# A state space layer whose score products are paired and whose segment inputs become one stream

## The chip, the cores and the metric

The program runs on one core of one Trainium2 chip. A core has TensorE (PE in the profile; its weight loads are listed as PEld), VectorE (DVE), ScalarE (ACT), GpSimd (POOL) and a queue engine SyncE (SP) that mainly issues DMAs. The metric is the time of one execution in device microseconds. "Granted clock" is the share of TensorE's full clock that the profile shows as granted.

## The reference

A hybrid layer works on `x` of 2 sequences x 1024 tokens x 512 features, in float32. Four blocks follow one another, each as `x = x + block(layernorm(x))`: a state space layer, a mixture of experts, an attention, and the same mixture again. The change concerns the state space layer:

```
xBCzA = einsum('bld,ed->ble', input_, in_proj_w)      # 2048 channels, 1024 gates, 64 time steps
xBC   = silu(causal_conv(xBC, 4 taps) + conv1d_bias)  # -> x (64 heads x 16), Bm, Cm (8 groups x 64)
dt    = softplus(A_log)
Lm    = exp(segsum(A))                                # decay between tokens of a chunk of 128
Y_diag = einsum('bcshn,bczhn,bhcsz,bczhp->bcshp', Cm, Bm, Lm, X)
states = ...                                          # carried from chunk to chunk
Y_off  = einsum('bcshn,bchpn,bhcs->bcshp', Cm, states, state_decay_out)
Du     = D[None, None, :, None] * x_in                # x_in = x / dt
```

The sum of these is multiplied by the silu of the gates `z` and projected back to 512 features. The mixture that follows has 8 experts of which each token takes two, and a shared part.

## The kernel before

The 2048 tokens are 16 chunks of 128 (`CHUNKS`). Two chunks form a segment of 256 tokens (`SEG`, `CPS = 2`), so there are 8 segments, four per sequence.

`segment_inputs` (L546) makes all that a segment's chunks need. It is a generator: each `yield` ends a step, and there are 27 (`INPUT_STEPS`). Its steps are: the LayerNorm of two token tiles, their transposes on TensorE and their copies into `xnT`, all in one step; the time steps (`ps_dt`, L563, and then a chain of about 15 small VectorE instructions, L572 to L593, the "dt chain"); the decays (`ps_cum`, `ps_row`), with the cumulative sums written to DRAM (`sums`); then 16 steps of four projection matmuls for a channel tile (`ps_ch`, L631), convolved by four VectorE instructions that read PSUM (L634, L638), and 8 steps for a gate tile (`ps_z`, L656, silu on ScalarE, L660). Projections share three PSUM banks (tag `proj`). Their weights `w_ch` come by SP in pairs of tiles, with three buffers.

`prologue(c)` (L687), in three steps, transposes a chunk's x and B, makes `xd` and `y` on GpSimd, adds the output of the former chunk's state, and makes the next state.

`scores(c)` (L767) multiplies B by C for all 8 groups into two PSUM tiles `g0` and `g1` and masks them.

`own(c, gs, between)` (L781) is a chunk's main part. It takes the 64 heads as 8 groups of 8, in two halves `e` of 4 groups. For one group, SP broadcasts a stretch of `sums` to all partitions (tile `m`, 512 KB, six buffers), GpSimd subtracts (L799), ScalarE does relu and exp (L801, L802), VectorE multiplies by the scores (L803), and TensorE does 8 products with 32 output rows each (`ps_y`, L807; the profile lists each float32 product as two instructions, so 16 per group). After each group there is a `yield`. When four groups are done, four more matmuls add `y` (L818) and VectorE multiplies by the gate into `yT` (L826). Both halves use one PSUM bank `y`. After the first half, `between` runs, which is the prologue of the next chunk. At the end come `scores(c + 1)` and the output projection `ps_out` (L833), which is added to x.

The loop at the end of the layer (L885) runs `own` step by step. With each step it adds `rate` to `due`, and for each whole unit it runs one step of `side`, the generator of the next segment's inputs. When a new segment is due, `before_chunk` runs `side` to its end and starts the next one. In the second sequence every other step also runs a step of `routes`: LayerNorm and router of the first sequence for the mixture, 8 tiles of 5 steps and then the routing itself.

The text order is not yet the order on the engines. The framework's planner orders each engine's instructions at compile time: it takes the earliest written instruction that by its own estimate is ready, gives out buffers and sets the waits. On the chip each engine then works in that fixed order. SP's DMAs stand in one queue, where one that waits for a buffer holds back those behind it.

At the start, `load_x` asks SP for the 8 tiles of the first sequence, ahead of all else. LayerNorm's statistics are VectorE instructions (L154, L155), the reciprocal root is GpSimd's (L158, L159), and the normalised tile `xn` VectorE's (L180).

Of the kernel before, what the change touches and what calls it, by code (L numbers as in the profile page):

```python
# [11 lines left out]
F32 = mybir.dt.float32  # L12
# [26 lines left out]
INPUT_STEPS = 3 + (NCH + DI) // P  # L39
CHUNK_STEPS = 12  # L40
# [48 lines left out]
def hybrid_layer_kernel(ctx: ExitStack, tc: tile.TileContext, a: dict, out: bass.AP):  # L89
# [14 lines left out]
    load_x(range(TPB))  # L104
# [26 lines left out]
    def count(shape, pattern, base, channel_multiplier, name):  # L131

        whole = ints.tile(shape, I32, name=name + "_i")
        nc.gpsimd.iota(whole, pattern=pattern, base=base, channel_multiplier=channel_multiplier)
        c = const.tile(shape, F32, name=name)
        nc.vector.tensor_copy(c, whole)
        return c
# [373 lines left out]
    with ExitStack() as sa:  # L511
# [15 lines left out]

        convw = wp.tile([P, NCH // P, TAPS], F32, name="convw")
# [7 lines left out]
        w_dt = wp.tile([P, KD, NH], F32, name="w_dt")  # L536
        nc.scalar.dma_start(out=w_dt, in_=a["wdt"])
# [8 lines left out]
        def segment_inputs(b, s, before):  # L546
# [5 lines left out]
            else:  # L552
                nc.gpsimd.tensor_copy(xnT[:, :, 0:HALO], before[:, :, SEG : SEG + HALO])
            for j in range(CPS):
                transposed(normalised(b, s * CPS + j, stats[j]), pp, "misc", xnT[:, :, HALO + j * P : HALO + (j + 1) * P])

# [13 lines left out]
            n = CPS * NH  # L570
            al = sp.tile([P, n], F32, tag="al", name="al", bufs=1)
            nc.vector.tensor_copy(al, ps_dt.rearrange("p c h -> p (c h)"))  # L572
            y = sp.tile([P, n], F32, tag="sp_y", name="sp_y", bufs=1)
            nc.vector.scalar_tensor_tensor(y, al, -1.0, al, ALU.mult, ALU.min)
            nc.scalar.activation(y, y, AF.Exp)
            r = sp.tile([P, n], F32, tag="sp_r", name="sp_r", bufs=1)
# [4 lines left out]
            s2 = sp.tile([P, n], F32, tag="sp_s2", name="sp_s2", bufs=1)  # L581
# [81 lines left out]
            for n, quad in enumerate((2, 3, 0, 1)):  # L663
                yield from channels(quad)
                yield from gates(n)
# [5 lines left out]
        for i in range(2):  # L671
            xc = wp.tile([P, NH // 2, 3, HP], F32, name=f"xc{i}")
            nc.gpsimd.memset(xc[:, :, 1, :], 0.0)
# [107 lines left out]
        def own(c, gs, between):  # L781


            b, s, j = place_of(c)
            cum, sums, gate = (segs[c // CPS][i] for i in (3, 4, 8))
            cols = slice(j * P, (j + 1) * P)
            xc = xcs[c % 2]
            y = started.pop(c)
            yT = cp.tile([P, 2, 4, P], F32, tag="wide", name="yT", bufs=4)
            for e in range(2):  # L790
                ps = pp.tile([P, 4, P], F32, tag="y", name="ps_y", bufs=1)
                for i in range(4):
                    h0 = (2 * i + e) * 8
                    m = cp.tile([P, 8, P], F32, tag="m", name="m", bufs=6)
                    nc.sync.dma_start(
                        out=m.rearrange("p h s -> p (h s)"),
                        in_=sums[j][h0 * P : (h0 + 8) * P].partition_broadcast(P),
                    )
                    nc.gpsimd.tensor_tensor(m, m, bc(cum[:, j, h0 : h0 + 8], 2, P), ALU.subtract)  # L799

                    nc.scalar.activation(m, m, AF.Relu)  # L801
                    nc.scalar.activation(m, m, AF.Exp, scale=-1.0)  # L802
                    nc.vector.tensor_tensor(m, m, bc(gs[e][:, i, :], 1, 8), ALU.mult)  # L803
                    for odd in range(2):
                        for quad in range(4):
                            hh = quad * 2 + odd
                            nc.tensor.matmul(  # L807
                                ps[quad * 32 : (quad + 1) * 32, i, :],
                                padded(xc, h0 + hh),
                                m[:, hh, :],  # L810
# [376 lines left out]
```

## Time and profile before

| | us |
|---|---|
| three runs, median (lowest to highest) | 2377.78 (2375.65 to 2384.19) |
| the profiled execution | 2371.49 |
| its span, first to last instruction | 2369.7 |
| granted TensorE clock, mean | 0.976 |
| end of the last `ps_out` of the state space layer | 812.9 |

The times of the profile are microseconds from the start of the span. A row of the timeline has the start, the length, engine, line, operation, what is written and read, the shape and how many instructions were joined; in brackets stands how long the engine was idle before it and what ended that. Consecutive matmuls overlap in these rows by about 0.1 us, so the time from one start to the next start is the measure of cost. A row of busy time by stretch has the stretch, its length, the busy time and number of instructions of PE, PEld, DVE, ACT and POOL, the granted clock, the busy share of the DMA engines, and GB/s. Where it is asked for PE alone, only PE stands there.

### The profile page before, as it was taken

The page shows a single profiled execution, that of the slowest core. Times are in us where ns is not written, and L with a number is a line of the kernel's source. Part 1 is how long each engine was busy: PE and PEld are TensorE (multiplying, and loading weights), DVE is VectorE, ACT ScalarE, POOL GpSimd, SP SyncE. Part 2 cuts the span into 40 slices and gives each one's busy share as a digit, 9 for nine tenths or more (in the row PEclk, how much of TensorE's full clock was granted, in tenths as well). Part 3 has the DMA queues.
Part 4 walks back from the last instruction along what each step waited for, and adds up shares of the span by engine and source line. Part 5 has one row for each costly group of instructions (what it writes and reads, how often), then busy time and mean ns, then how long its engine had stood idle before and what let it go on. Part 6 is the DMA issues. An engine that isn't in the chain of part 4 may idle for free.

```text
span 2369.7 us, 29938 instructions
## 1 busy us (share of the span) xinstructions
PE 2237.8 (94%) x10996; PEld 1445.1 (61%) x10996; DVE 1418.6 (60%) x2117; ACT 860.9 (36%) x1416; POOL 1100.2 (46%) x757
## 2 busy tenths in 40 slices
PE   7999999999999999999889999999899998889998
PEld 6766767676776565655556556556556554556654
DVE  6867777777676530012249989884699899710002
ACT  4656576666566422211222223221223322212221
POOL 3443454455646300002377887744788886110002
PEclk9999999999999999999999999999999999989999
DMA  7444554454555487876744463344565553378775
GB/s 262 155 145 147 164 177 151 137 191 144 174 170 193 163 268 258 299 258 218 254 146 166 162 230 132 131 153 165 199 237 200 180 179 123 119 261 291 281 265 156
DMA packets 119314, 456.42 MB, mean 193 GB/s; under 512 B 17281, under 2 KB 20097, under 8 KB 106369
## 3 DMA queue, kind: packets, MB, share of 16 engines
q1 hardware_dynamic: 91904, 387.03, 47.0%
q0 software_dynamic: 12480, 40.90, 5.6%
q10 hardware_dynamic: 14784, 26.58, 3.1%
q8 instruction: 88, 1.44, 0.2%
q14 instruction: 58, 0.47, 0.1%
HBM read 408.84 MB, written 45.61 MB: 192 GB/s over the span
## 4 chain that ended last, share of the span: by engine, by line
PE 65%; DVE 11%; POOL 9%; DMA 6%; ACT 5%; issue 3%; POOLq 0%; ACTq 0%; SPq 0%; DVEq 0%
PE ps_o L470 13%; PE ps_u L448 11%; PE ps_g L439 11%; PE ps_ch L631 6%; PE ps_out L833 5%; POOL pr L1005 4%; PE ps_z L656 3%; DMA m<-sums 2%; PE ps_xnT L186 2%; PE ps_y L807 2%; POOL m L799 2%; DVE sc L1009 2%; PE ps_ao L1041 2%; DMA part<-made,r_slots 2%; DVE pv L1025 2%
## 5 line engine op out<-in xcount | busy, mean ns | idle before, releaser
L1005 POOL TENSOR_TENSOR pr<-qk 128x1536 f32<-128x1536 f32 x128 | 440.7, 3459 | 85.9 <-DVE sc L1009 55.3
L799 POOL TENSOR_TENSOR m<-m,cum 128x1024 f32<-128x1024 f32 x128 | 243.2, 1908 | 327.9 <-DMA m<-sums 215.9
L449 DVE TENSOR_TENSOR h<-h,ps_u 128x352 f32<-128x352 f32 x156 | 80.6, 517 | 493.3 <-PE ps_u L448 484.8
L376 POOL DMA_INDIRECT xg<-normed,r_tok x92 | 89.8, 976 | 531.5 <-PE ps_xnT L186 461.9
L631 PE MATMUL ps_ch<-xnT,w_ch 128*128 128x259 f32 x1024 | 263.1, 404 | 12.9 <-DVE chan L638 12.0
L470 PE MATMUL ps_o<-w_d,hT 128*128 128x512 f32 x552 | 257.9, 601 | 6.7 <-ACT hT L462 6.7
L1009 DVE TENSOR_REDUCE sc<-pr 128x32 f32<-128x1536 f32 x128 | 224.4, 1753 | 50.6 <-POOL pr L1005 50.6
L439 PE MATMUL ps_g<-w_gu,xT 128*128 128x352 f32 x736 | 238.1, 463 | 1.1 <-DMA w_gu<-in_wall 0.9
L448 PE MATMUL ps_u<-w_gu,xT 128*128 128x352 f32 x736 | 236.6, 462 | 0.0
L441 ACT ACTIVATE h<-ps_g 128x352 f32<-128x352 f32 x156 | 72.4, 464 | 449.0 <-PE ps_g L439 443.7
L631 PEld LDWEIGHTS ps_ch<-xnT,w_ch 128*128 128x128 f32 x1024 | 194.5, 197 | 61.2 <-issue 28.8
L801 ACT ACTIVATE m<-m 128x1024 f32<-128x1024 f32 x128 | 134.5, 1054 | 198.7 <-POOL m L799 198.5
L439 PEld LDWEIGHTS ps_g<-w_gu,xT 128*128 128x128 f32 x736 | 138.1, 191 | 93.5 <-issue 35.6
L476 ACT COPY y<-ps_o 128x512 f32<-128x512 f32 x92 | 53.9, 586 | 376.7 <-PE ps_o L470 376.7
L470 PE MATMUL ps_o<-s_d,hT 128*128 128x512 f32 (+1 forms) x384 | 182.1, 606 | 4.6 <-DVE x L473 3.8
L638 DVE SCALAR_TENSOR_TENSOR chan<-ps_ch,convw,chan 128x256 f32<-128x256 f32 x384 | 181.7, 478 | 7.5
L470 PEld LDWEIGHTS ps_o<-w_d,hT 128*128 128x128 f32 x552 | 105.8, 193 | 115.2 <-issue 88.1
L448 PEld LDWEIGHTS ps_u<-w_gu,xT 128*128 128x128 f32 x736 | 133.6, 192 | 60.9 <-issue 4.9
L439 PE MATMUL ps_g<-s_gu,xT 128*128 128x352 f32 x512 | 169.4, 464 | 0.6 <-ACT h L441 0.6
L448 PE MATMUL ps_u<-s_gu,xT 128*128 128x352 f32 x512 | 165.4, 461 | 0.0
L803 DVE TENSOR_TENSOR m<-m,g 128x1024 f32<-128x1024 f32 x128 | 150.9, 1215 | 19.8 <-ACT m L802 19.5
L1025 DVE TENSOR_TENSOR pv<-sc,vT 128x1024 f32<-128x1024 f32 x128 | 155.9, 1218 | 1.1
(211 smaller groups left out, 3548.5 us busy)
## 6 DMA issues: line engine op xcount, KB each, us to landing
w_gu<-in_wall SPq DMA_DIRECT2D x92, 1408.0 KB, 7.8
w_d<-in_wall SPq DMA_DIRECT2D x92, 768.0 KB, 4.6
m<-sums SPq DMA_DIRECT2D x128, 512.0 KB, 4.8
w_ch<-in_wch SPq DMA_DIRECT2D x96, 512.0 KB, 4.1
made<-y ACTq DMA_DIRECT2D x92, 256.0 KB, 6.0
xT<-columns SPq DMA_DIRECT2D x64, 256.0 KB, 5.0
s_gu<-in_wall SPq DMA_DIRECT2D x7, 1408.0 KB, 6.7
normed<-xn SPq DMA_DIRECT2D x32, 256.0 KB, 2.4
```

Of the source, the lines that this page charges most:

```text
L439: nc.tensor.matmul(ps_g, xT[:, k, :], both[:, k, 0, :], start=(k == 0), stop=(k == KD - 1))
L448: nc.tensor.matmul(ps_u, xT[:, k, :], both[:, k, 1, :], start=(k == 0), stop=(k == KD - 1))
L470: nc.tensor.matmul(ps_o, hT[:hn, c, :], wd[:hn, c, :], start=(c == 0), stop=(c == len(HC) - 1))
L631: nc.tensor.matmul(ps, w[:, ct % 2, k], xnT[:, k, :], start=(k == 0), stop=(k == KD - 1))
L638: nc.vector.scalar_tensor_tensor(c[:, i], ps[:, tap : tap + SEG], convw[:, ct, tap : tap + 1], c[:, i], ALU.mult, ALU.add)
L799: nc.gpsimd.tensor_tensor(m, m, bc(cum[:, j, h0 : h0 + 8], 2, P), ALU.subtract)
L801: nc.scalar.activation(m, m, AF.Relu)
L803: nc.vector.tensor_tensor(m, m, bc(gs[e][:, i, :], 1, 8), ALU.mult)
L833: nc.tensor.matmul(ps_out, yT[:, e, i, :], w_out[:, 2 * i + e, :], start=(e == 0 and i == 0), stop=(e == 1 and i == 3),)
L1005: nc.gpsimd.tensor_mul(pr, bc(qks[t][:, 0, i : i + IC, :], 2, AH), bc(qks[t][:, 1], 1, IC))
L1009: nc.vector.tensor_reduce(scores[t][:, i : i + IC, :], products.pop((t, i)), AX.X, ALU.add)
L1025: nc.vector.tensor_tensor(pv, bc(scores[t][:, i : i + IC, :], 2, DH), bc(vs[t], 1, IC), ALU.mult)
```

## The change

Four things are changed in the state space layer.

`own` is rewritten around runs of two groups, four runs to a chunk. `decayed(c, n)` makes the two tiles `m` of run n; `from_scores(c, n)` does the 32 score instructions of that run in one go. `decayed` is called one run ahead, so run 0 of chunk c + 1 is made in chunk c, and `scores(c + 1)` moves ahead of the last run of chunk c. A chunk now has 16 steps instead of 12.

The inputs of all segments are chained to one stream `side`. `before_chunk` no longer empties it, it only makes sure that the segment is there. By the first turn of a segment the stream is six steps (`LEAD`) further. LayerNorm becomes a step of its own, ahead of the transposes.

At the start, two tiles of x are asked for instead of eight; the six others come when the first segment's steps have reached number 10, the second sequence as before after that. `w_dt` is the first on ScalarE's DMA queue instead of the last. 22 transposes of the identity (`WARM`) go to TensorE ahead of the stream.

Four small casts go from VectorE to GpSimd, and two memsets of `xcs` from GpSimd to VectorE.

```diff
-INPUT_STEPS = 3 + (NCH + DI) // P
-CHUNK_STEPS = 12
+INPUT_STEPS = 4 + (NCH + DI) // P
+CHUNK_STEPS = 16
+LEAD = 6
+WARM = 22
...
-    load_x(range(TPB))
+    load_x(range(CPS))
...
-        nc.vector.tensor_copy(c, whole)
+        nc.gpsimd.tensor_copy(c, whole)
...
+        w_dt = wp.tile([P, KD, NH], F32, name="w_dt")
+        nc.scalar.dma_start(out=w_dt, in_=a["wdt"])
         convw = wp.tile([P, NCH // P, TAPS], F32, name="convw")
...
-        def segment_inputs(b, s, before):
+        def segment_inputs(b, s, before, n):
...
+            rows_before[n] = xnT
+            xns = [normalised(b, s * CPS + j, stats[j]) for j in range(CPS)]
+            yield
+
             for j in range(CPS):
-                transposed(normalised(b, s * CPS + j, stats[j]), pp, "misc", xnT[:, :, HALO + j * P : HALO + (j + 1) * P])
-
+                transposed(xns[j], pp, "misc", xnT[:, :, HALO + j * P : HALO + (j + 1) * P])
             yield
...
-            nc.gpsimd.memset(xc[:, :, 1, :], 0.0)
+            nc.vector.memset(xc[:, :, 1, :], 0.0)
...
+        def decayed(c, n):
+            cum, sums = segs[c // CPS][3:5]
+            j = c % CPS
+            ready[c, n] = []
+            for i in (n % 2 * 2, n % 2 * 2 + 1):
+                e = n // 2
+                h0 = (2 * i + e) * 8
+                m = cp.tile([P, 8, P], F32, tag="m", name="m", bufs=6)
+                nc.sync.dma_start(
+                    out=m.rearrange("p h s -> p (h s)"),
+                    in_=sums[j][h0 * P : (h0 + 8) * P].partition_broadcast(P),
+                )
+                nc.gpsimd.tensor_tensor(m, m, bc(cum[:, j, h0 : h0 + 8], 2, P), ALU.subtract)
+                nc.scalar.activation(m, m, AF.Relu)
+                nc.scalar.activation(m, m, AF.Exp, scale=-1.0)
+                nc.vector.tensor_tensor(m, m, bc(raw[c][e][:, i, :], 1, 8), ALU.mult)
+                ready[c, n].append(m)
+                yield
+
+        def from_scores(c, n):
+            ...
+            for i, m in zip((n % 2 * 2, n % 2 * 2 + 1), ready.pop((c, n))):
+                for odd in range(2):
+                    for quad in range(4):
+                        hh = quad * 2 + odd
+                        nc.tensor.matmul(
+                            ps[quad * 32 : (quad + 1) * 32, i, :],
+                            padded(xc, (2 * i + e) * 8 + hh),
+                            m[:, hh, :],
+                            ...
+                        )
+            if n % 2 == 1:
+                ...
+                nc.vector.tensor_tensor(finished[c][:, e], ps, gate[e][:, :, j * P : (j + 1) * P], ALU.mult)
...
+        def own(c, between):
+            finished[c] = cp.tile([P, 2, 4, P], F32, tag="wide", name="yT", bufs=4)
+            for n in range(4):
+                if n < 3:
+                    yield from decayed(c, n + 1)
+                elif c + 1 < CHUNKS:
+                    raw[c + 1] = scores(c + 1)
+                    yield from decayed(c + 1, 0)
+                from_scores(c, n)
+                yield
+                if n == 1:
+                    yield from between
+            project_out(c)
+            yield
...
-        for _ in inputs(0):
-            pass
+        warm = pp.tile([P, 4, P], F32, tag="y", name="warm", bufs=1)
+        for i in range(WARM):
+            nc.tensor.transpose(warm[:, i % 4], ident, ident)
+
+        side = chain(*(inputs(n) for n in range(CHUNKS // CPS)))
+        for n in range(INPUT_STEPS):
+            next(side)
+            if n == 10:
+                load_x(range(CPS, TPB))
...
-        gs = scores(0)
-        side = inputs(1)
-
-        rate = INPUT_STEPS / (CHUNK_STEPS + CHUNK_STEPS // 2 - 2)
+        raw[0] = scores(0)
+        for _ in decayed(0, 0):
+            pass
+        rate = (INPUT_STEPS + LEAD) / (CHUNK_STEPS + 6)
         due = 0.0
...
                 if c % CPS == 0:
-                    for _ in side:
-                        pass
-                    n = c // CPS + 1
-                    side = inputs(n) if n * CPS < CHUNKS else iter(())
+                    while c // CPS not in segs:
+                        next(side)
                     rate = INPUT_STEPS / (CPS * CHUNK_STEPS)
-                    due = 0.0
                 yield from prologue(c)
```

## The prediction

> **What bounds the kernel now.** I read the page first, then the state space part (roughly the first 815 us) in stretches, then TensorE's waits, then single places of the timeline. The page, and the table of busy time by stretch (60:740 is the steady part, 740:815 its tail, the rest is the later layers):
>
> ```profile
> span 2369.7 us, 29938 instructions
> PE 2237.8 (94%) x10996; PEld 1445.1 (61%) x10996; DVE 1418.6 (60%) x2117; ACT 860.9 (36%) x1416; POOL 1100.2 (46%) x757
> 0.00:60.00 60.00, 44.58 (x190) 37.90 (x191) 37.69 (x100) 27.06 (x31) 18.07 (x31) 0.97 0.77 261
> 60.00:740.00 680.00, 646.98 (x4788) 477.27 (x4787) 500.18 (x876) 428.12 (x491) 335.41 (x233) 0.98 0.48 159
> 740.00:775.00 35.00, 27.97 (x229) 17.27 (x226) 24.69 (x27) 20.88 (x25) 24.85 (x14) 0.87 0.61 223
> ```
>
> TensorE sets the time: in 60:740 it is busy 647 of 680 us, VectorE 500, ScalarE 428, GpSimd 335. So the change can win only idle TensorE time (33 us there), clock not granted, and busy time that is not multiplication. Places where each shows (start, length, engine, line; what a pause waited for):
>
> ```profile
> 11.13 1.00 DVE L180 TENSOR_SCALAR xn<-x,mv,rstd 128x512 f32<-128x512 f32 x2
> 11.73 1.97 PE L186 MATMUL ps_xnT<-ident,xn 128*128 128x128 f32 x8 [11.73 <-DVE xn L180]
> 13.52 3.68 PE L563 MATMUL ps_dt<-w_dt,xnT 128*128 128x64 f32 x16
> 16.99 9.52 PE L631 MATMUL ps_ch<-xnT,w_ch 128*128 128x259 f32 x32
> 31.33 7.17 PE L631 MATMUL ps_ch<-xnT,w_ch 128*128 128x259 f32 x32
> ...
> 79.64 3.33 PE L631 MATMUL ps_ch<-xnT,w_ch 128*128 128x259 f32 x14
> 82.90 0.64 PE L807 MATMUL ps_y<-m,xc 128*32 128x128 f32 x16
> ...
> 329.16 0.64 PE L807 MATMUL ps_y<-m,xc 128*32 128x128 f32 x16
> 329.74 2.02 PE L631 MATMUL ps_ch<-xnT,w_ch 128*128 128x259 f32 x8
> 331.69 0.64 PE L807 MATMUL ps_y<-m,xc 128*32 128x128 f32 x16
> ...
> 446.15 1.75 DVE L574 SCALAR_TENSOR_TENSOR sp_y<-al 128x128 f32<-128x128 f32 x1
> 446.74 5.53 PE L631 MATMUL ps_ch<-xnT,w_ch 128*128 128x259 f32 x24
> 455.25 3.60 PE L631 MATMUL ps_ch<-xnT,w_ch 128*128 128x259 f32 x8 [2.99 <-DVE chan L638]
> 747.39 1.95 PE L807 MATMUL ps_y<-m,xc 128*32 128x128 f32 x64
> ...
> 455.10:458.50 3.40, 3.25 (x8) 0.50 0.01 2
> ```
>
> To be seen: TensorE starts at 11.73; the same 32 matmuls take 9.52 us at first and 7.17 later; score products (ps_y) alternate with projections (ps_ch); when a segment begins, ps_ch waits for VectorE, and the 8 matmuls after that pause take 3.60 instead of 2.02 at a granted clock of 0.50.
>
> **The change part by part.** The sum is against the profiled execution: 2371.49 us, 1.79 more than its span. The median of three runs, 2377.78, is 6.29 higher; I carry the difference over to it.
>
> *Start.* Tile 0's statistics begin at 3.66 and both tiles' are done by 5.42, but GpSimd holds the next step (L159, 9.18) behind the statistics of a tile that lands later. With two tiles asked for, L159 (0.70 for two columns) can follow L158 at 5.8, xn (0.53) at 6.5, and TensorE at 7.1 instead of 11.73: 4.6 us. Four casts (0.15 to 0.22 each on VectorE) go to GpSimd and two memsets (0.97 for both) leave it; its constants end at 3.5, so they lie ahead of L158. SP issued eight x tiles for 5.98 us ahead of the first w_ch (6.84); now two, some 1.5 us. The other six come behind the fourth w_ch, which waits for a buffer; VectorE first needed tiles 2 and 3 for the next segment at 30.25; uncovered they would cost one landing, about 4 us. w_dt goes from last to first on ScalarE's queue, 2.84 us earlier, hidden. Ends 2 and 4.6; I take 4.
>
> The 22 warming transposes (eight took 1.97, so 5.4 us) fit between ident at 1.5 and 7.1. They could give back the slow start: 16 ps_dt took 3.68 at first and 1.27+0.88 for 10 and 6 later, less 0.1 overlap each; with 9.52-7.17 that is 1.6+2.3=3.9. Ends 0 and 3.9; I take 3. **Start: -7.**
>
> *Two groups in a run.* A score group alone takes 329.74-329.16=0.58; four in a run take 749.27-747.39=1.88. So a group costs 0.43 and a run 0.15 on top. Projections: 14 between two score groups take 82.90-79.64=3.26, 8 take 331.69-329.74=1.95; so 0.218 each and 0.20 per block. One switch less saves 0.35 us. There are 16 chunks x 8 = 128 groups, so at most 64 merges, 22 us; around each prologue groups already join (30 and 24 in the rows after 346), and there prologue matmuls may still cut a run. Ends 0 (other work cuts every run) and 22; I take 48 merges, near the upper end, because most runs in the timeline hold one group (91 of 123, counted): **-17**.
>
> *One run ahead, stream six steps ahead.* The matmuls are the same. Idle in 60:740 is 680-646.98=33 us. Clock: half in 171.8 to 175.2, 250.3 to 253.7, 352.7 to 359.5, 455.1 to 458.5, 533.6 to 537.0, 554.1 to 557.5, 642.8 to 649.6, together 30.6 us, so 15 lost. Together 48, nearly all within 25 us behind a segment's turn. There the flush of the old stream, LN, transposes, dt chain and the prologue come together: VectorE has both yo and the dt chain, GpSimd xd, y, state and m. After the change LN and dt are due 4 to 7 yields before that prologue, and projections are left as cover beside it; LN on VectorE gets a step of its own ahead of its transposes. What stays: the dt chain still stands ahead of the convolutions on VectorE, and ps_ch has three banks. That wait alone is 12.0 us of the 33. Ends 0 and 48 won; nor is a loss excluded, since one more pause as at 455 (2.99 and 1.7 of clock) per segment turn is 7x4.7=33. I take half of it, **-24**: the waits for ACT and POOL results in the prologue go, those for VectorE's chain stay. Late next is the dt chain.
>
> One rule weighs against this. The Trainium skill, "SBUF — State Buffer", section "SBUF: two separate sides", says that VectorE and GpSimd take turns at a shared port pair, whole instructions long. The trace agrees: L574 took 1.75 us beside a GpSimd subtraction, its shortest is 0.29. By the rule the chain is as slow wherever GpSimd subtracts; an estimate by it alone is half of this part, -12, and a sum of -34. Another rule, "TensorE: Matmul & The Clock Gate", section "What's actually happening", puts half clock behind an idle window of about 3.4 us; here 1.2 us before 352.7 was enough. By that rule only the 4.8 us pause before 171.96 would cost clock, 1.7 instead of 15, so this part would be half of 35 and the sum -39; the measurement decides.
>
> *New waits.* A run stands on TensorE until both m are multiplied; behind it wait projections, and on VectorE the convolutions wait behind an m that is late. Chain for one m: landing 4.8, L799 1.9, L801 and L802 2.1, table 1.28, L803 1.2 = 11.3. Six buffers hold three runs; at 11 us a run (45 per chunk) that is some 22 us of lead. Nothing, as long as queueing stays under ten.
>
> *Tail.* The stream ran out in chunk 13's first half; it now ends after chunk 12 (34 steps in 22 yields, then 0.875 each: yield 207 of 16 per chunk). Routing moves on every second yield and a chunk has 16 instead of 12, so it ends in chunk 13 instead of 15. Chunks 13 to 15 have GpSimd's 8x1.90+1.93+1.93+2x1.28+2x1.06=23.7 against TensorE's 7.1+3.8+2.1+1.8+1.2+1.6+1.1=18.7: up to 5 idle each, 15. Against that the present tail already idles 7.0 in 740:775, and later layers' ps_g moved in at 781. Ends -7 and +15; **+2**.
>
> Sum: -7-17-24+2=-46; 2371.5-46=2325.5, on the median **2332 us**.
>
> **The rivals.** *Turns stay as they are* (the DVE chain and port hold the 48 us): -7 and 8 to 17 of the switches, tail worse by 2 to 8: about 2362. For it: the 12.0 us wait; against: prologue waits that a lead must shorten. *Everything goes*: -8-22-40-7=-77, 2301; against it the same wait. *Slower: a run's second m is late.* GpSimd already waited 215.9 us for m to land, landings took up to 10.1. If TensorE stands before each run, 64 runs, gains of 46 are gone at 0.72 us each; at 1.2 us with its clock it ends near 2410. Against: ps_y waited only 2.2 us in all. *The order isn't what the text says*: instructions here are ordered by a planner (ps_ch of one block stand in 6 and 2 around ps_out), which could cut runs: then -29, 2349, inside my range.
>
> **How the numbers follow.** Forecast, with cut runs: 0.66, own range 2306 to 2358. Turns stay: 0.15 (2350 to 2372, a third of it above 2366). Everything goes: 0.07. Slower: 0.12, of it 0.02 within 0.5%. Half a per cent, 12 us, is about what a measurement here can tell. Faster 0.66+0.10+0.07=0.83, same 0.05+0.02=0.07, slower 0.10. Range 2300 to 2368: it leaves out the slower case and about half of the largest gain and a little of the second.
>
> **What would show it.** First PE matmul besides warm ones near 7 us, 32 ps_ch in 7.2 us; ps_y in runs of 32; ps_ch's wait for VectorE around 6 to 12 us; fewer half-clock stretches between 60 and 700; the last ps_out 46 us earlier than 812.9, with what follows as long as now. I am wrong if ps_y waits for m in most chunks, if runs are cut, or if the tail from the last ps_ch on idles over 20 us.

## The result and the profile after

The changed kernel takes 2408.49 us (median of four runs, 2397.56 to 2411.54); the kernel before 2376.72 (median of four, 2370.18 to 2384.19). The ratio is 1.0124, with a 95% interval of 1.008 to 1.0168: about 30 us slower (1.2%), where 46 us less were forecast. The profiled execution took 2409.57, with a span of 2407.4, 37.7 above the span before.

From the page after, TensorE's granted clock in tenths (40 slices of 60 us):

```profile
PEclk9999999999996899999999999999999999989999
```

The clock line has a dent in its thirteenth and fourteenth slices, 720 to 840 us: the end of the state space layer. Busy time by stretch after, all engines, in the columns of the prediction's table:

```profile
60.00:740.00 680.00, 620.97 (x4688) 467.09 (x4686) 486.34 (x870) 430.32 (x489) 319.85 (x229) 0.98 0.49 156
740.00:775.00 35.00, 22.91 (x156) 19.15 (x156) 20.57 (x37) 15.24 (x17) 21.24 (x12) 0.54 0.37 127
```

In 60:740 TensorE has 26 us less to do (646.98 before) and stands still for 59 us instead of 33. In 740:775 it has half its clock.

Fixed stretches compare unlike work, so the rest of this text cuts the run at two events: the end of the input stream (the last `ps_ch` or `ps_z`) and the end of the layer (the last `ps_out`). The same view, for TensorE alone, from 60 to the first event and from there to the second. Before:

```profile
60.00:726.50 666.50, 634.73 (x4638) 0.98 0.48 159
726.50:812.90 86.40, 78.12 (x645) 0.90 0.45 159
```

After:

```profile
60.00:732.90 672.90, 615.73 (x4576) 0.98 0.49 155
732.90:838.50 105.60, 83.54 (x667) 0.74 0.40 137
```

The stream ends 6.4 us later, the tail is 19.2 longer, and what follows the layer takes 1568.9 instead of 1556.8, 12.1 more. These three make the 37.7. In the first stretch idle time rose from 31.8 to 57.2, busy time fell by 19.0; the clock there stayed as it was (30.7 us at half clock both times). In the tail idle time rose by 13.8 and busy time by 5.4.

**New waits in the steady part.** What ended TensorE's idle time in 60:740 after (engine, operation, line, what it waited for: total, times, longest):

```profile
PE ps_ch L636 <- ACT gate L665: 16.3, 6, 3.9
PE ps_z L661 <- issue: 12.6, 5, 3.4
...
PE ps_ch L636 <- DVE chan L643: 3.5, 1, 3.5
```

Before, the last of these and the first read:

```profile
PE ps_ch L631 <- DVE chan L638: 12.0, 6, 4.8
...
PE ps_ch L631 <- ACT gate L660: 0.9, 2, 0.5
```

The wait that the list puts down to VectorE's convolutions fell, from 12.0 to 3.5, and a wait for ScalarE's gates came. But the five waits of `ps_z` for which the list names nothing ("issue", 12.6 us) belong to VectorE too: each ends 0.10 us after a convolution of VectorE's that stands right behind a step of the dt chain. The one at 355.70, in the timeline after:

```profile
354.93 0.27 DVE L591 SCALAR_TENSOR_TENSOR sp_r<-sp_r,sp_s 128x128 f32<-128x128 f32 x1
355.13 0.47 DVE L643 SCALAR_TENSOR_TENSOR chan<-ps_ch,convw,chan 128x256 f32<-128x256 f32 x1
...
355.70 1.97 PE L661 MATMUL ps_z<-xnT,w_ch 128*128 128x256 f32 x8 [2.10 <-issue]
```

With these, and with 6.1 us in which the transposes of `xnT` wait for the addition of `ps_out` to x (L853), all of TensorE's waits for VectorE up to the stream's end come to 22.7 us, where the kernel before had 21.9. What is new is ScalarE: 16.3 us for its gates (0.9 before) and 15.6 for its other results (7.2 before). One of the six waits for the gates, in the timeline after:

```profile
309.43 1.06 ACT L805 ACTIVATE m<-m 128x1024 f32<-128x1024 f32 x1 [3.41 <-POOL m L803]
311.29 1.06 ACT L805 ACTIVATE m<-m 128x1024 f32<-128x1024 f32 x1 [0.80 <-POOL m L803]
...
313.31 1.28 ACT L647 ACT_TABLE_LOAD   x1
...
315.56 0.82 ACT L665 ACTIVATE gate<-ps_z,zb 128x256 f32<-128x256 f32 x2
316.07 3.70 PE L636 MATMUL ps_ch<-xnT,w_ch 128*128 128x259 f32 x8 [3.17 <-ACT gate L665]
```

ScalarE works through its instructions in a fixed order. It stands for 3.41 and 0.80 us at the relu of tiles `m` that GpSimd has not subtracted yet (GpSimd has just worked on `xd` and `y` of the prologue, from 303.71 to 307.5); the silu of two gate tiles stands behind them; so two of the three projection banks stay full, and TensorE waits 3.17 us for one and runs the next eight matmuls in 3.70 us instead of about 2.

**The tail.** Timeline after, from the end of the stream:

```profile
733.00 1.95 PE L823 MATMUL ps_y<-m,xc 128*32 128x128 f32 x64
...
737.06 1.08 PE L823 MATMUL ps_y<-m,xc 128*32 128x128 f32 x32
748.74 1.08 PE L823 MATMUL ps_y<-m,xc 128*32 128x128 f32 x16 [10.60 <-DVE m L807]
```

GpSimd and SP's queue in the same place:

```profile
733.70 6.47 SPq L799 DMA_DIRECT2D m<-sums  x6
741.64 11.17 POOL L803 TENSOR_TENSOR m<-m,cum 128x1024 f32<-128x1024 f32 x6 [12.56 <-DMA m<-sums]
```

In about 5 us TensorE uses up the six tiles that stood ready. All six buffers are then asked for anew within 6.5 us, and TensorE stands 10.6 us for the first. Its clock falls to half and stays there; busy time and clock of TensorE in two stretches:

```profile
742.80:780.30 37.50, 26.39 (x182) 0.50 0.40 134
783.80:800.80 17.00, 14.74 (x87) 0.50 0.20 63
```

In these 54.5 us TensorE is busy for 41.1; by estimate half of that, 20.6 us, is due to the clock. The tail before has 17.0 us of half clock with 14.7 busy, so 7.4. The clock then costs some 13 us more than before, beside the 13.8 us of idle time.

### The profile page after: what moved, and what is told of

Read it like the earlier page. It is cut to its first block, busy times and chain, and to the rows that moved or that the text cites. A ratio compares the mean times of both kernels' runs of the same rounds, so it can differ in the third digit from the quotient of the medians.

```text
span 2407.4 us, 29968 instructions
## 1 busy us (share of the span) xinstructions
PE 2244.0 (93%) x11018; PEld 1464.5 (61%) x11018; DVE 1417.2 (59%) x2115; ACT 869.8 (36%) x1420; POOL 1100.2 (46%) x759
## 4 chain that ended last, share of the span: by engine, by line
PE 61%; DVE 11%; POOL 10%; DMA 7%; ACT 6%; issue 5%; SPq 0%; POOLq 0%; ACTq 0%; DVEq 0%
PE ps_o L472 12%; PE ps_u L450 11%; PE ps_g L441 11%; PE ps_ch L636 6%; POOL pr L1035 4%; DMA m<-sums 4%; PE ps_out L845 3%; PE ps_z L661 3%; PE ps_xnT L188 2%; DVE sc L1039 2%; POOL m L803 2%; DVE pv L1055 2%; PE ps_ao L1071 2%; PE ps_y L823 2%; DVE o L1056 2%
## 5 line engine op out<-in xcount | busy, mean ns | idle before, releaser
L636 PE MATMUL ps_ch<-xnT,w_ch 128*128 128x259 f32 x1024 | 258.4, 399 | 22.9 <-ACT gate L665 16.5
```

Of the source, the lines that this page charges most:

```text
L636: nc.tensor.matmul(ps, w[:, ct % 2, k], xnT[:, k, :], start=(k == 0), stop=(k == KD - 1))
```

## The experiments

Part of the change was undone, or done alone on the kernel before. "Points" are hundredths of the time before, from the ratios; the table after the last experiment has all numbers. Each kernel has one profiled execution, and that can lie up to 11 us from the kernel's median, so differences of a few us between two traces say little by themselves.

**The stream's lead taken back** (after):

```diff
-LEAD = 6
+LEAD = 0
```

> The changed kernel with LEAD = 0: the stream no longer runs six steps ahead at a segment's turn, all else as changed. Theory T (the loss is in the last three chunks, which have no filler left): the stream lasts seven steps of the loop longer, so the tail is shorter by under half a chunk: about 2395 to 2400 us, and the pause of 10.6 us before ps_y near 748 stays. Rival L (the lead puts gate tiles beside the prologue, where ScalarE stands behind late m tiles): TensorE's wait of ps_ch for the gates falls from 16.5 us to under 5 and the time to about 2385.

2408.11 us, ratio 1.0112 [1.0087, 1.0138]: no difference to the change, and neither theory's time; only the fall of the wait for the gates came as the rival had it. The waits are others. TensorE's, 60:740:

```profile
PE ps_ch L636 <- DVE chan L643: 16.8, 7, 7.0
PE ps_ch L636 <- DVE sp_r L589: 14.9, 3, 7.8
PE ps_z L661 <- DVE chan L643: 9.4, 5, 3.8
...
PE ps_ch L636 <- ACT gate L665: 3.2, 3, 2.3
```

Without the lead, and with the run ahead, TensorE waits 41 us for VectorE (its dt chain and the convolutions behind it) and little for the gates. Whether that is the lead's merit shows only without the run ahead, further below.

**Routing of the mixture at 3/8 instead of 1/2 of the steps** (after). A chunk has 16 steps instead of 12, so at an unchanged pace per step the routing ends earlier: its last products (`ps_t`) end 36 us ahead of the layer's last `ps_out`, where in the kernel before they end 4 us ahead of it. This run restores the pace per chunk (6 router steps).

```diff
-                    turn += 1
-                    if turn % 2 == 0:
+                    turn += 3
+                    if turn >= 8:
+                        turn -= 8
```

> The changed kernel with the routing steps at 3 in 8 loop steps instead of 1 in 2, which is the pace per chunk of the kernel before, so that they last into chunk 15. Theory T: they fill the last chunks again, the half-clock stretch of 37.5 us behind 742 breaks up, 2383 to 2395 us. Rivals L (lead) and D (the runs of two disturb all along): no change, 2400 to 2412.

2398.20, ratio 1.0075 [1.0052, 1.0099]: 0.5 points less than the change, a time between the two forecasts. The tail is 93.8 instead of 105.6:

```profile
60.00:742.50 682.50, 624.91 (x4546) 0.95 0.47 151
742.50:836.30 93.80, 80.75 (x711) 0.89 0.48 163
```

In the tail the idle time falls from 22.1 to 13.0 us and the clock rises from 0.74 to 0.89, with work left to lay beside the last `m`. But ahead of the stream's end the clock is worse (0.95 for 0.98): over both stretches the half clock lasts 85 us here and 85 after the change, so it has moved, not gone. The stream ends 9.6 us later and the layer only 2 earlier; most of the gain is behind the layer (1562.2 for 1568.9), where 32 instructions of the mixture's first matmuls had already been done before the layer's end, against 12 after the change and 28 before it.

**The start alone** (on the kernel before):

```diff
-    load_x(range(TPB))
+    load_x(range(CPS))
...
-        for _ in inputs(0):
-            pass
+        for i in range(WARM):
+            nc.tensor.transpose(warm[:, i % 4], ident, ident)
+        for n, _ in enumerate(inputs(0)):
+            if n == 10:
+                load_x(range(CPS, TPB))
```

with `w_dt` first and the casts and memsets moved.

> The kernel before with the start alone: two tiles of x first, w_dt first, the 22 warming transposes, the casts and memsets moved. All theories: first real matmul near 8 us instead of 11.7; if later waits absorb nothing, 4 to 8 us less, 2369 to 2373; if the conv chain on VectorE paces the first segment anyway, the same as before.

2374.70, ratio 0.9982 [0.9964, 1.0001]: some 4 us faster, with an interval that reaches to nothing. TensorE's start in this run:

```profile
1.50 4.34 PE L863 MATMUL warm<-ident 128*128 128x128 f32 x22 [1.50 <-POOL ident masks.py:199]
7.95 1.53 PE L187 MATMUL ps_xnT<-ident,xn 128*128 128x128 f32 x8 [2.10 <-DVE xn L181]
9.28 3.68 PE L564 MATMUL ps_dt<-w_dt,xnT 128*128 128x64 f32 x16
12.75 6.75 PE L632 MATMUL ps_ch<-xnT,w_ch 128*128 128x259 f32 x24
21.83 3.48 PE L632 MATMUL ps_ch<-xnT,w_ch 128*128 128x259 f32 x8 [2.33 <-DVE chan L639]
```

The first real matmul comes 3.8 us earlier (11.73 before). The eight transposes of `xn` take 1.53 us instead of 1.97; beyond that the warming gave nothing: `ps_dt` takes 3.68 as before, 24 `ps_ch` take 0.28 us each (0.30 before, 0.22 at full clock), and a pause of 2.33 for VectorE, which the kernel before did not have here, is followed by eight more slow ones. The new start without warming was not run.

**The pairs alone** (on the kernel before; a group is held until its partner is ready):

```diff
+                held = []
...
-                    for odd in range(2):
-                        ...
+                    held.append((i, h0, m))
+                    for i_, h_, m_ in held if i % 2 else ():
+                        for odd in range(2):
+                            ...
+                    if i % 2:
+                        held = []
```

> The kernel before with the pairing alone: both m tiles of a pair are made, then their 32 matmul instructions follow in one go; no run ahead, no lead, old start. If a switch costs 0.35 us, as the timeline's rows say: 12 to 20 us less, 2357 to 2365. Rival D (pairing itself makes waits, since a run stands until its second tile is ready): 2377 or more, with ps_y waiting for VectorE over 10 us in all.

2375.40, ratio 0.9995 [0.9975, 1.0015]: nothing, where 2357 to 2365 was expected if a switch costs 0.35 us. Yet TensorE has less to do, to the end of the stream:

```profile
60.00:723.90 663.90, 624.19 (x4637) 0.98 0.50 159
```

That is 10.5 us less busy time than before for one instruction less, and the stream ends 2.6 us earlier: 7.9 of the 10.5 came back as idle time. The waits say where (60:740):

```profile
PE ps_ch L631 <- DVE chan L638: 6.9, 4, 4.5
PE ps_b L708 <- ACT xc L702: 6.3, 5, 1.7
PE ps_x L701 <- ACT chan L642: 5.1, 5, 1.2
PE ps_ch L631 <- ACT gate L660: 4.6, 4, 1.3
```

A TensorE that is done sooner waits longer for ScalarE: its results up to the stream's end cost TensorE 20.5 us instead of 8.1, GpSimd's 3.7 instead of 1.3, while the wait for VectorE falls from 21.9 to 15.3.

**Pairs and start together** (on the kernel before; both edits above, nothing else):

```diff
+    load_x(range(CPS))
+                    for i_, h_, m_ in held if i % 2 else ():
```

> The kernel before with pairing and the new start together; no run ahead, no lead. Alone they gave 0.9995 and 0.998 of the time before. If the pauses at the segments' turns set the pace and take back what TensorE saves, they don't add up: 2368 to 2378. If each only lost its gain by chance, 2355 to 2365. Theory B (run ahead is what costs, since finished m tiles hold buffers) expects no loss here: at most 2378.

2368.91, ratio 0.9971 [0.9947, 0.9994]: 7 us faster than before. So the changed kernel's loss is not in these two parts; it lies in what this run lacks: the run ahead, the one stream with its lead and order, LayerNorm as a step of its own, and the 16 steps.

**Eight buffers for `m`** (after). Room comes from half of the output projection's weights, each used twice.

```diff
-                m = cp.tile([P, 8, P], F32, tag="m", name="m", bufs=6)
+                m = cp.tile([P, 8, P], F32, tag="m", name="m", bufs=8)
...
-                        w_out[:, 2 * i + e, :],
+                        w_out[:, (2 * i + e) % 4, :],
```

> The changed kernel with eight m buffers instead of six. The room comes from w_out, of which only half is loaded and each half used twice, so the output projection is computed with the wrong half of its weights; the number and size of its matmuls stay. Theory B (buffers: a run that is finished and waits holds two of six, so loads start late): GpSimd's wait for m tiles falls from 298 us towards 216, the pause of 10.6 us near 748 goes, 2380 to 2392 us. Theory T (no filler in the last chunks) and L (ScalarE's order): 2400 or more, the half-clock stretch stays.

2403.87, ratio 1.0118 [1.0082, 1.0153]: no measurable difference. GpSimd's wait for `m` to land falls from 271.1 to 229.1 us and TensorE's wait for a multiplied `m` (60:840) from 12.9 to 0.9; the tail still has 37.5 us of half clock. The layer ends 17.6 us earlier in this trace (820.9), but what follows takes 8 longer (1577.2). More buffers alone do not mend it.

**No run ahead** (after; the stream, its lead and the pairs stay):

```diff
-                if n < 3:
-                    yield from decayed(c, n + 1)
-                elif c + 1 < CHUNKS:
-                    raw[c + 1] = scores(c + 1)
-                    yield from decayed(c + 1, 0)
+                yield from decayed(c, n)
                 from_scores(c, n)
```

with `scores(c + 1)` at the chunk's end as in the kernel before.

> The changed kernel without the run ahead: the m tiles of a run are made directly before its products, scores for the next chunk stand at the end of a chunk as before; pairs, lead, stream, start and routing as changed. Theory B: the loss shrinks to what the tail without routing costs, 2378 to 2392. If lead and tail alone are to blame, it stays at 2400 to 2410. If the run ahead helped, it is slower than 2410.

2394.71, ratio 1.0086 [1.0055, 1.0118]: 0.4 points less than the change, between two of the forecasts. GpSimd's wait for `m` to land, 60:840, is 271.1 us after the change, 188.5 without the run ahead, and 185.9 in the kernel before: a finished tile that lies a run ahead keeps its buffer, and the next broadcast is asked for only when TensorE has used it. That wait by itself is no loss, though: the pairs alone, which lose nothing, have 241.0.

Idle time up to the stream's end is still 53.6 us, and the wait for the gates is as long as after the change (18.4). The pause shown above is here too, without a run ahead, in the same lengths:

```profile
305.69 1.06 ACT L805 ACTIVATE m<-m 128x1024 f32<-128x1024 f32 x1 [3.41 <-POOL m L803]
...
312.33 2.02 PE L636 MATMUL ps_ch<-xnT,w_ch 128*128 128x259 f32 x8 [3.17 <-ACT gate L665]
```

So the run ahead is not what makes TensorE wait for the gates.

**No run ahead, routing at 3/8** (after; both edits):

```diff
+                yield from decayed(c, n)
...
+                    turn += 3
```

> The same without the run ahead, and with routing at 3 in 8 steps, so that the last chunks have filler as before. B and T together: both losses gone, 2362 to 2378, level with the kernel before or a little faster. If the lead costs by itself (L), 2385 or more.

2394.21, ratio 1.0062 [1.0036, 1.0087]. The two gains don't add up here: the time is above 2385, as expected if the lead costs by itself. The tail is as short as with the slow routing alone, and the stream ends at 734.8.

**No run ahead, no lead** (after):

```diff
-LEAD = 6
+LEAD = 0
...
+                yield from decayed(c, n)
```

> The changed kernel without run ahead and with LEAD = 0. So far: ahead and lead 2408, ahead without lead 2408, lead without ahead 2395. If both cost (ahead through late loads, lead through gate tiles beside a prologue): 2375 to 2385, with ps_ch's wait for the gates under 6 us and its wait for VectorE near the 12 us of the kernel before. If the stream's finer pace (16 steps a chunk, LayerNorm as its own step, routing sooner) is what costs: 2390 to 2400.

2387.49, ratio 1.0037 [1.0014, 1.006], idle to the stream's end 39.5; the time lies between the two forecasts. Of the four combinations, run ahead and lead are worth nothing or a loss: 2408 (both), 2408 (run ahead alone), 2395 (lead alone), 2387 (neither). TensorE's waits from 60 us to the stream's end, added up from the list (the unnamed waits of `ps_z` counted with VectorE):

| kernel | for VectorE | for ScalarE's gates | for other results of ScalarE |
|---|---|---|---|
| before | 21.9 | 0.9 | 7.2 |
| both (the change) | 22.7 | 16.3 | 15.6 |
| run ahead alone | 48.0 | 3.2 | 6.8 |
| lead alone | 23.7 | 18.4 | 9.5 |
| neither | 22.9 | 4.5 | 10.5 |

The wait for the gates comes with the lead, whether there is a run ahead or not. And the lead shortens the wait for VectorE only where the run ahead has made it long; without the run ahead that wait is 22.9 us without the lead and 23.7 with it.

"Neither" is still 0.7 points above pairs and start, with intervals apart. What it has beyond them (16 steps with the sooner routing, LayerNorm as a step of its own, scores and products in another order) was not taken apart.

**Gate tiles apart** (after). The stream has its gate tiles in twos between fours of channel tiles; here two times four channel tiles come first.

```diff
-            for i, quad in enumerate((2, 3, 0, 1)):
-                parts += [channels(quad)] * 4 + [gates(i)] * 2
+            for part, times in (
+                (channels(2), 4), (channels(3), 4), (gates(0), 2), (gates(1), 2),
+                (channels(0), 4), (channels(1), 4), (gates(2), 2), (gates(3), 2),
+            ):
+                parts += [part] * times
```

> The changed kernel with only the order of the stream's tiles altered, so that no gate tile falls due beside a prologue: eight channel tiles, four gate tiles, and the same again. Theory L (ScalarE stands behind relu of an m that GpSimd has not subtracted, the gate's silu stands behind it, and its PSUM bank is held): the wait of ps_ch for the gates falls from 16 us to under 6 and the time to 2385 to 2398. If VectorE's chain then stops TensorE in the same places: 2405 to 2410.

2394.49, ratio 1.0084 [1.0053, 1.0114]: 0.4 points less than the change, as expected. The wait of `ps_ch` for the gates falls from 16.3 to 1.3 us and the stream ends 16 us earlier (716.6). TensorE's longest waits now, 60:740 (the first of them already is the tail's):

```profile
PE ps_y L826 <- DVE m L810: 10.3, 1, 10.3
PE ps_ch L636 <- issue: 9.7, 5, 3.1
PE ps_ch L636 <- DVE chan L643: 5.9, 4, 3.5
```

The order of the tiles, and with it ScalarE's queue, was the cause of that wait. The five at "issue" end 0.10 us behind a convolution here too. The tail is hardly better, 100.9.

**Gate tiles late, on pairs and start** (on the kernel before with those two parts; not the same order as in the last run):

```diff
-            for n, quad in enumerate((2, 3, 0, 1)):
-                yield from channels(quad)
-                yield from gates(n)
+            for part in (
+                channels(2), gates(0), channels(3), channels(0),
+                gates(1), channels(1), gates(2), gates(3),
+            ):
+                yield from part
```

> Pairs and the new start on the kernel before, and the order of its tiles altered so that the last channel tiles come four steps sooner and the last gates at the end. If waits of the prologue for the last channels (4.5 us) and for the gates (4.3 us) go: 2360 to 2366 instead of 2369. If they are given back elsewhere: 2367 to 2373.

2368.44, ratio 0.9969 [0.9948, 0.999]: as without it. The wait for the gates was only 4.3 us there and falls to 0.7, but the prologue's wait for ScalarE (`ps_b` for `xc`) rises from 7.1 to 10.1, and idle time is 39.7 us for 40.4: it was given back elsewhere.

**Eight buffers and routing at 3/8** (after; both edits):

```diff
+                m = cp.tile([P, 8, P], F32, tag="m", name="m", bufs=8)
...
+                    turn += 3
```

> The changed kernel with eight m buffers (w_out half loaded and used twice, so that the output projection has wrong weights) and routing at 3 in 8 steps. Alone the buffers gave 2404 and the routing 2398. If the last three chunks lose by both, that is by m tiles that empty together and by missing filler: the tail from the stream's end to the last ps_out falls from 105.6 to 85 us and the time to 2380 to 2390. If not, 2395 or more.

2387.04, ratio 1.0044 [1.0021, 1.0066]: 0.8 points less than the change, where the buffers alone gave 0.1 and the pace alone 0.5. GpSimd's wait for `m` is 180.6 us, as before the change, and the tail 86.9. With eight buffers the slower routing gains 0.7 points, and there the intervals are apart: that the routing's pace costs time is proven here. What the buffers add to the slower routing (1.0075 to 1.0044) is not, since those intervals overlap. Eight buffers with all of the weights were not run.

**Three causes taken away together** (after; no run ahead, gate tiles apart, routing at 3/8; pairs, stream, lead and start stay):

```diff
+                (channels(2), 4), (channels(3), 4), (gates(0), 2), (gates(1), 2),
+                (channels(0), 4), (channels(1), 4), (gates(2), 2), (gates(3), 2),
...
+                yield from decayed(c, n)
...
+                    turn += 3
```

> The changed kernel with three causes taken away together: no run ahead, gate tiles apart from the prologues, routing at 3 in 8 steps; pairs, the stream six steps ahead and the start stay. If the causes are separate and add up (about 13, 14 and 10 us of the 32 lost): 2368 to 2380, level with the kernel before or better. If they hide one another (whatever is taken away, the next wait takes its place): 2385 to 2395.

2367.31, ratio 0.9957 [0.9939, 0.9975]: faster than the kernel before, and 1.7 points below the change. Busy time and clock of TensorE from the stream's end, at 708.4, to the layer's:

```profile
708.40:804.40 96.00, 85.22 (x706) 0.86 0.45 160
```

The dent in the clock is mostly gone: 0.86 in the tail, where the change has 0.74 and the kernel before 0.90. The longest wait, 60:740, is the old one:

```profile
PE ps_ch L636 <- DVE chan L643: 10.1, 5, 2.7
```

**A shorter dt chain** (with the gate tiles apart; five of the seven steps of the series left out, so the time steps are less exact):

```diff
-            for c in ATANH[-2:0:-1]:
+            for c in ATANH[2:0:-1]:
```

> The changed kernel with gate tiles apart, and five of the seven steps of the series in the dt chain left out (so dt is less exact). If VectorE's dt chain makes the pauses at a segment's turn (ps_ch without a named releaser 9.7 us, and for VectorE 5.9 us): these fall by half or more, and the time from 2394 to 2380 to 2388. If the chain is paced by GpSimd at the shared port or by the PSUM banks, five instructions of 0.28 us change little: 2390 to 2398.

2382.71, ratio 1.0026 [1.0001, 1.0051], 0.6 points less than with the gates apart alone. The waits at the turn fell only a little: `ps_ch` at "issue" from 9.7 to 9.0, `ps_ch` for the convolutions from 5.9 to 3.4. So the chain costs time (the intervals are just apart), but most of the 12 us can't be put to a wait in the list; the two profiled executions differ by only 3.3 us, so it stays open.

All results (median; ratio; then from the one profiled execution the end of the stream, TensorE's idle time from 60 to it, the tail to the layer's end, and the time behind the layer; nothing was changed there, and it varies with the half clock as well as with what had moved in before):

| kernel | us | ratio [95%] | stream end | idle | tail | behind |
|---|---|---|---|---|---|---|
| before | 2376.72 | 1 | 726.5 | 31.8 | 86.4 | 1556.8 |
| after | 2408.49 | 1.0124 [1.008, 1.0168] | 732.9 | 57.2 | 105.6 | 1568.9 |
| no lead | 2408.11 | 1.0112 [1.0087, 1.0138] | 738.4 | 61.7 | 98.5 | 1580.6 |
| routing 3/8 | 2398.20 | 1.0075 [1.0052, 1.0099] | 742.5 | 57.6 | 93.8 | 1562.2 |
| start alone | 2374.70 | 0.9982 [0.9964, 1.0001] | 720.2 | 32.2 | 90.7 | 1562.8 |
| pairs alone | 2375.40 | 0.9995 [0.9975, 1.0015] | 723.9 | 39.7 | 84.2 | 1561.0 |
| pairs, start | 2368.91 | 0.9971 [0.9947, 0.9994] | 718.4 | 40.4 | 83.5 | 1564.0 |
| eight buffers | 2403.87 | 1.0118 [1.0082, 1.0153] | 726.6 | 53.7 | 94.3 | 1577.2 |
| no run ahead | 2394.71 | 1.0086 [1.0055, 1.0118] | 726.8 | 53.6 | 97.2 | 1565.6 |
| no run ahead, routing 3/8 | 2394.21 | 1.0062 [1.0036, 1.0087] | 734.8 | 58.1 | 94.3 | 1562.9 |
| no run ahead, no lead | 2387.49 | 1.0037 [1.0014, 1.006] | 724.7 | 39.5 | 95.3 | 1574.5 |
| gates apart | 2394.49 | 1.0084 [1.0053, 1.0114] | 716.6 | 40.1 | 100.9 | 1564.7 |
| pairs, start, gates late | 2368.44 | 0.9969 [0.9948, 0.999] | 721.3 | 39.7 | 85.1 | 1566.6 |
| eight buffers, routing 3/8 | 2387.04 | 1.0044 [1.0021, 1.0066] | 734.6 | 57.3 | 86.9 | 1572.6 |
| three causes | 2367.31 | 0.9957 [0.9939, 0.9975] | 708.4 | 35.4 | 96.0 | 1560.7 |
| gates apart, short chain | 2382.71 | 1.0026 [1.0001, 1.0051] | 710.8 | 39.6 | 101.8 | 1566.3 |

The intervals of the three single cures (routing, no run ahead, gates apart) overlap that of the change, so by time alone none of them is proven on its own; each rests on its trace. Together they are proven: 0.9975 is far below 1.008. Singly they give 0.5, 0.4 and 0.4 points, together 1.7; whether that is more than their sum, the intervals don't tell. And "three causes", "pairs, start" and "pairs, start, gates late" can't be told apart: the one stream with its lead adds nothing that is measured to the pairs and the start.

## Why the prediction was wrong

**The step that failed is "One run ahead, stream six steps ahead", -24.** Idle time up to the stream's end rose by 25.4 us instead of falling, and the half clock there stayed as long as it was. The prediction took half of the 48 us of pauses and lost clock as a gain, because LayerNorm and the dt chain would be due earlier and projections would be left as cover beside the prologue. The trace does not show that gain: TensorE waited for VectorE 22.7 us, 21.9 before, and the lead by itself changed nothing in it (23.7 with, 22.9 without). The waits for ScalarE's results, of which the step said that those in the prologue would go, rose from 8.1 to 31.9 us in all. Of the rise, 15.4 us are the gates: the lead puts gate tiles beside the prologue, where their silu stands on ScalarE behind the relu of tiles that GpSimd delivers late, and the projection banks stay full. That queue, and through it the banks, was not in the prediction's list of what is queued behind what, which named VectorE's convolutions and TensorE. Three runs show it: the wait goes when the lead goes (3.2 us), goes when the gate tiles are moved (1.3), and stays when the run ahead goes (18.4). Where the other 8.4 us for ScalarE come from was not traced. The upper bound of loss (33 us, seven turns of one more pause each) would have held the outcome; the value taken had the wrong sign. The two other estimates of the prediction (sums of -34 and -39) kept that sign and missed as well.

**"New waits", "Nothing, as long as queueing stays under ten", failed too.** It counted six buffers as 22 us of lead. A run made ahead keeps two of them until its turn, and GpSimd's wait for landings grew by 85 us (185.9 to 271.1). In 60:740 it didn't reach TensorE as a wait for `m`: the list shows none there. In the tail it did, once, where all six came free together (10.60 us).

**The tail, "+2", was 19 us in the tail itself and 12 behind it.** Its end +15 is near the idle time that came (+13.8), by luck: it was worked out from GpSimd's work being longer than TensorE's in every one of the last chunks, and most of what came is one wait of 10.60 us for tiles that all had to be loaded anew. One of the signs of being wrong that the prediction named did come: the tail idled 22.1 us, over 20. What the step did not price is the clock, which made the tail's work some 13 us longer than before. That routing ends early was seen in the prediction ("in chunk 13 instead of 15"), but only as an order of events, not as cover taken from the last chunks. It also set the 12 us behind the layer in part: 16 fewer instructions of the mixture had moved in, at some 0.30 us each from start to start (eight `ps_u` take 2.37 us from 844.67 on) 4.7 us. Nearly all the rest is the clock behind the layer, where TensorE is busy at half clock for 53.7 us after and 40.3 before: by the same estimate 6.7 us more.

**"Two groups in a run", -17: the mechanism was right, the gain did not arrive.** The trace after has 83 runs of `ps_y` where there were 123, so 40 switches fewer rather than 48; at 0.35 us each that is 14. The pairs alone took 10.5 us of busy time away, and 7.9 of it came back as pauses, mostly for ScalarE. The step treated TensorE's busy time in the whole layer as the path; where another engine's result is due right behind it, it is not.

**"Start", -7: 3.7 of the 4 us for the earlier start came; the 3 us for the clock did not.** The first real matmul stood at 8.06 rather than 7.1. The statistics were done 0.4 us later than before (5.79 for 5.42), and three of the casts moved to GpSimd stand between the two halves of the reciprocal root, not ahead of both as the step had it:

```profile
5.88 0.27 POOL L160 TENSOR_SCALAR rstd<-mv 128x2 f32<-128x2 f32 x1 [3.12 <-DVE quarters L204]
...
6.15 0.28 POOL L138 CAST place<-place_i 128x128 f32<-128x128 int32 x1
6.38 0.19 POOL L138 CAST block_of<-block_of_i 128x23 f32<-128x23 int32 x1
6.52 0.19 POOL L138 CAST block_at<-block_at_i 128x23 f32<-128x23 int32 x1
6.69 0.73 POOL L161 TENSOR_TENSOR rstd<-rstd,minus_half 128x2 f32<-128x2 f32 x1
```

**The rivals.** The slower one had the time nearly right (about 2410), by luck: its mechanism is wrong, for TensorE did not stand before each run, but waited for `m` 12.9 us in all (60:840), 10.6 of it once. "The order isn't what the text says" did not decide: 31 runs have exactly 32 instructions, and the runs became fewer.

**The port rule** was right about the chain. At one turn after the change (timeline):

```profile
350.68 3.79 POOL L803 TENSOR_TENSOR m<-m,cum 128x1024 f32<-128x1024 f32 x2 [1.22 <-DMA m<-sums]
350.78 1.87 DVE L589 TENSOR_SCALAR sp_r<-sp_s 128x128 f32<-128x128 f32 x1
...
352.97 1.64 DVE L591 SCALAR_TENSOR_TENSOR sp_r<-sp_r,sp_s 128x128 f32<-128x128 f32 x1
```

The two slow steps end at 352.65 and 354.61, within 0.15 us of the ends of GpSimd's two subtractions of 1.9 us (352.6 and 354.5); the next, at 354.93, takes 0.27. The convolution behind it is the one that `ps_z` waits for at 355.70. This is what the Trainium skill, "SBUF — State Buffer", section "SBUF: two separate sides", says of the shared pair of ports: it is held for a whole instruction. The lead moved the chain, but not out of GpSimd's way.

## What to carry to other kernels

Work that is moved must be followed along every queue that it enters, past what stands ahead of it there, and along every buffer that it then keeps: here silus moved beside a prologue stood behind the relu of a late tile that had nothing to do with them, and kept TensorE's banks full. A wait for which a list names nothing should be looked up in the timeline before a wait is said to have fallen. When the number of steps in a loop changes, whatever is paced by steps changes its pace too, and filler work that ends early uncovers the loop's last rounds. A gain in the busy time of the busiest engine counts only where no other engine is due right behind it; measure it alone before adding it to a sum.

## What the runs showed of the hardware

Half clock lasted longer here than the stretches of 3.4 to 6.8 us in the steady part of the kernel before. In the tail it held for 37.5 us. TensorE's 26.39 busy ones all lie behind the pause that ends at 748.74, in the last 31.6 of them, where no pause was longer than 2 us. At the start after the change the warming transposes ended at 6.1, TensorE paused for 1.97 us, ran eight transposes in 1.18 us (1.97 before), and the clock was at half from 9.0 to 15.8, in a stretch almost without a pause (TensorE's row of busy time):

```profile
9.00:15.80 6.80, 6.65 (x25) 0.50 1.04 403
```

The Trainium skill, "TensorE: Matmul & The Clock Gate", section "What's actually happening", puts half clock behind an idle window of about 3.4 us and full clock behind as long a busy one. Here a pause of 1.97 us was followed by half clock, and 6.65 us of work in 6.80 passed before it was full again: less idleness was enough, and more work was needed.
